# Tail of a fused two-layer graph network: bias on GpSimd, statistics and verdict ahead of the aggregation's copies, last evictions in another order

## Chip, cores and metric

The kernel runs on one core of a Trainium2 chip. The metric is the device time of one launch in microseconds, as the median of several runs. Engines are named as in the profile: PE is TensorE (PEld its weight loads), DVE is VectorE, ACT is ScalarE, POOL is GpSimd, SP is SyncE, which issues the DMAs here. A "q" behind an engine's name is its instruction queue.

## What is computed

The input is 32 graphs of 512 nodes with 512 features each. Layer 0 is masked attention with 8 heads of 64, layer 1 is a graph convolution with a dense 512 x 512 adjacency. Both add their input and normalise each node's features to mean 0 and variance 1.

```python
def _L0_gnn_ref(x, adj, Wq, bq, Wk, bk, Wv, bv):
    ...
    scores = jnp.einsum('bihd,bjhd->bhij', q, k) / jnp.sqrt(jnp.float32(HD))
    mask = jnp.where(adj == 0, jnp.float32(-1000000000.0), jnp.float32(0.0))
    scores = scores + mask[None, None, :, :]
    weights = jax.nn.softmax(scores, axis=-1)
    out = jnp.einsum('bhij,bjhd->bihd', weights, v)
    ...
def _L1_gnn_ref(x, adj, weight, bias):
    y = jnp.einsum('nm,bmd->bnd', adj, x)
    out = jnp.einsum('bnd,do->bno', y, weight) + bias
...
x = _layernorm(x + _L0_gnn_ref(x, adj, L0_gnn_Wq, L0_gnn_bq, L0_gnn_Wk, L0_gnn_bk, L0_gnn_Wv, L0_gnn_bv), axis=-1)
x = _layernorm(x + _L1_gnn_ref(x, adj, L1_gnn_weight, L1_gnn_bias), axis=-1)
```

## The kernel before

Batch b is one graph, held as `X[b]`: 128 partitions, four blocks of rows (c = 0 to 3), 512 features. While batch b is in its attention, the projections of b + 1 and the graph convolution of b - 1 and b - 2 are woven into it; the program's order is written out by hand, so each engine runs its instructions in the order in which the code issues them, and waits on semaphores for its inputs. Only the end is of interest here, where nothing is left to weave in. There t = 31 is the last batch, and batch 30 is the one before it.

The matrix product with the weight in layer 1 is done by Strassen's scheme in seven products (units 1, 2, 5, 6, 7, 3, 4 in this order, 8 matmuls each). The function `convolve(b, i)` runs unit i and adds its bank of PSUM into quarters of `X[b]`: x11, x12 (left and right half of blocks 0 and 1), x21, x22 (of blocks 2 and 3). Unit 1 is also copied to a tile `mix` by ScalarE (L535); units 6 and 7 add their bank to `mix` on VectorE (L537), and GpSimd then adds `mix` to x12, and to x21 and x22 (L539). All other additions are on VectorE from PSUM (L541).

The end of the program, from L803 on, runs as follows.

- The last units of batch 30 are mixed with the normalisation of layer 0 of batch 31. For each block, ScalarE normalises (L446) and copies the rounded high part (L502), and VectorE subtracts it from the row for the low part (L503). `split_rows` does the latter two.
- `add_bias` (L506) adds the bias of layer 1 to each of the four blocks, in place, on VectorE.
- `aggregate_rows` multiplies with the adjacency: 32 matmuls into four banks (L515), which ScalarE (L522, banks 0 and 2) and VectorE (L520, banks 1 and 3) copy to the tile `yT`. VectorE adds one more combination from banks 2 and 3 (L524), and GpSimd makes three further ones (`combine_rows`, L331 to L333).
- The list `last` then runs the seven units of batch 31. Beside them, by the table `beside`, run `seen` (the statistics of layer 1 of batch 30, L431 and L432, one pair for each block) and `old` (its normalisation: square root on ScalarE, L435; reciprocal and shift on VectorE, L440 and L441; four normalisations on ScalarE, L446). The finished batch 30 is stored by one DMA after unit 7 (L472).
- `judge` (L663 to L673) computes on VectorE whether all numbers stayed in range: three sums (L665 to L667), two comparisons (L669, L670) and two products (L671, L672). A matmul sums the outcome over the partitions at the very end (L859), and VectorE writes the verdict (L860).
- `half_statistics` (L832) computes the statistics of a half row of batch 31, and L849 merges two halves. Blocks 0 and 1 are finished after unit 3, blocks 2 and 3 after unit 4; each pair then gets its square root, reciprocal, shift, normalisation on ScalarE and a store for each block (L470).

After that each engine loads the verdict into a register (L201) and branches on it (L203). If it says so, a slower general kernel runs; otherwise the program closes with a barrier over all engines (shown at L881).

Of the kernel before, what the change touches and what calls it, by code (L numbers as in the profile page):

```python
# [37 lines left out]
FP = mybir.dt.float32  # L38
# [4 lines left out]
ALU = mybir.AluOpType  # L43
# [4 lines left out]
P = 128  # L48
# [16 lines left out]
def load_row(nc, pool, v, name):  # L65
    t = pool.tile([P, v.shape[0]], FP, name=name)
    nc.sync.dma_start(t, bass.AP(tensor=v.tensor, offset=v.offset, ap=[[0, P], [1, v.shape[0]]]))
    return t
# [139 lines left out]
def fast_kernel(ctx: ExitStack, tc, verdict, x, adj, Wq, bq, Wk, bk, Wv, bv, W1, b1, out):  # L208
    nc = tc.nc
    B, N, D = x.shape  # L210
    H = Wq.shape[1] // HD
    HP = H // 2
    NB = N // P
# [5 lines left out]
    work = ctx.enter_context(tc.tile_pool(name="work", bufs=2))  # L219
# [3 lines left out]
    def bank(*shape):  # L223

        return psum.tile([P, *shape], FP, name="bank", tag="bank", bufs=8)


    X, IN = {}, {}
    half = N // 2
# [40 lines left out]
    b1_r = load_row(nc, consts, b1, "b1_r")  # L270
# [57 lines left out]
    def combine_rows(t):  # L328

        a11, a12, a21, _, s1, s2, s4 = (t[:, i, :, :] for i in range(7))  # L330
        nc.gpsimd.tensor_sub(s2, s1, a11)  # L331
        nc.gpsimd.tensor_sub(a21, a11, a21)
        nc.gpsimd.tensor_sub(s4, a12, s2)  # L333
# [28 lines left out]
    def block_product(pm, t, w, i, turned=False):  # L362
        left, right = FACTORS[i]
        left, right = t[:, A_AT[left], :, :], w[:, B_AT[right], :, :]
        if turned:
            left, right = right, left
        for r in range(2):
            for d in range(2):
                nc.tensor.matmul(pm[:, r, :], left[:, d, r * P:(r + 1) * P], right[:, d, :],  # L369
                                 start=(d == 0), stop=(d == 1))  # L370
# [52 lines left out]
    STAT, RSTD, SHIFT, HIGH, LOW = {}, {}, {}, {}, {}  # L423
# [10 lines left out]
    def square_root(t, slots):  # L434
        nc.scalar.activation(RSTD[t][:, slots], STAT[t][:, slots, 1], AF.Sqrt, bias=eps)  # L435

    def invert_root(t, slots):

        rstd = RSTD[t][:, slots]
        nc.vector.reciprocal(rstd, rstd)  # L440
        nc.vector.scalar_tensor_tensor(SHIFT[t][:, slots], STAT[t][:, slots, 0], -1.0, rstd,  # L441
                                       op0=ALU.mult, op1=ALU.mult)

    def normalise(t, slot):
        row = X[t - slot // NB][:, slot % NB, :]
        nc.scalar.activation(row, row, AF.Identity, bias=SHIFT[t][:, slot:slot + 1],  # L446
                             scale=RSTD[t][:, slot:slot + 1])
# [20 lines left out]
    def store(b, blocks=None):  # L468
        for c in blocks or ():
            nc.sync.dma_start(out[b, c * P:(c + 1) * P, :], X[b][:, c, :])  # L470
        if blocks is None:
            nc.sync.dma_start(out[b].rearrange("(c p) d -> p c d", p=P), X[b])  # L472
# [6 lines left out]
    YT, MIX = {}, {}  # L479
# [23 lines left out]
        nc.vector.tensor_sub(low, row, high.bitcast(FP))  # L503

    def add_bias(b, c):
        nc.vector.tensor_add(X[b][:, c, :], X[b][:, c, :], b1_r)  # L506

    def aggregate_rows(b):

        yt = YT[b] = work.tile([P, 7, 2, half], FP, name="yT", bufs=1)  # L510
        banks = [bank(2, half) for _ in range(DB)]
        for c in range(NB):
            for d, pm in enumerate(banks):
                for part in (LOW[b, c], HIGH[b, c]):
                    nc.tensor.matmul(pm.rearrange("p a n -> p (a n)"), part[:, d * P:(d + 1) * P], adjT[:, c, :],  # L515
                                     start=(c == 0 and part is LOW[b, c]), stop=(c == NB - 1 and part is HIGH[b, c]))
        for d, pm in enumerate(banks):
            block = yt[:, d // 2:d // 2 + 3:2, d % 2, :]
            if d % 2:
                nc.vector.tensor_copy(block, pm)  # L520
            else:
                nc.scalar.activation(block, pm, AF.Copy)  # L522
            if d >= 2:
                nc.vector.tensor_add(yt[:, A_AT["S1"], d % 2, :], pm[:, 1, :], yt[:, A_AT["A21"], d % 2, :])  # L524
        combine_rows(yt)

    def convolve(b, i):

        pm = bank(2, half)
        block_product(pm, YT[b], w1, i)  # L530
        x11, x12, x21, x22 = (X[b][:, 2 * r:2 * r + 2, s * half:(s + 1) * half] for r in range(2) for s in range(2))
        if i == 1:

            MIX[b] = work.tile([P, 2, half], FP, name="mix", tag="q" if b >= B - 3 else "low", bufs=2)
            nc.scalar.activation(MIX[b], pm, AF.Copy)  # L535
        if i in (6, 7):
            nc.vector.tensor_add(MIX[b], pm, MIX[b])  # L537
            for block in (x12,) if i == 6 else (x21, x22) if b == B - 1 else (x22,):
                nc.gpsimd.tensor_add(block, block, MIX[b])  # L539
        for block in {1: (x11,), 5: (x12, x22), 2: (x11,), 3: (x12,), 4: (x21,)}.get(i, ()):  # L540
            nc.vector.tensor_add(block, pm, block)  # L541
        if i == 4 and b < B - 1:

            nc.gpsimd.tensor_add(x21, x21, MIX[b])
# [6 lines left out]
    def convolution(b):  # L551
        return [(convolve, b, i) for i in (1, 2, 5, 6, 7, 3, 4)] if b >= 0 else []
# [110 lines left out]
    def judge():  # L663
        seen = consts.tile([P, 3], FP, name="seen")
        nc.vector.tensor_reduce(seen[:, 0:1], sums, axis=AX.XY, op=ALU.add)  # L665
        nc.vector.tensor_reduce(seen[:, 1:2], inverses, axis=AX.XY, op=ALU.add)
        nc.vector.tensor_reduce(seen[:, 2:3], inexact, axis=AX.X, op=ALU.add)  # L667
        well = consts.tile([P, 3], FP, name="well")
        nc.vector.tensor_scalar(well[:, 0:2], seen[:, 0:2], BOUND, None, op0=ALU.is_le)  # L669
        nc.vector.tensor_scalar(well[:, 2:3], seen[:, 2:3], 0.0, None, op0=ALU.is_equal)  # L670
        nc.vector.tensor_mul(well[:, 0:1], well[:, 0:1], well[:, 1:2])  # L671
        nc.vector.tensor_mul(well[:, 0:1], well[:, 0:1], well[:, 2:3])  # L672
        return well[:, 0:1]  # L673


    def run(units):
        for unit in units:
            unit[0](*unit[1:])
# [15 lines left out]
    def norm(t, which):  # L694

        if t - which < 0:
            return []
        lo, hi = which * NB, (which + 1) * NB
        return [(square_root, t, slice(lo, hi)), (invert_root, t, slice(lo, hi))] + [
            (normalise, t, slot) for slot in range(lo, hi)]  # L700
# [4 lines left out]
    def survey(b):  # L705

        return [(statistics, b, 1, c) for c in range(NB)] if b >= 0 else []
# [95 lines left out]
    t = B - 1  # L803
# [4 lines left out]
    old, seen = norm(t - 1, 1), survey(t - 1)  # L808
# [11 lines left out]
    run(rest[3 + NB:])  # L820
    for c in range(NB):
        add_bias(t, c)
    aggregate_rows(t)


    halves = {}
    spare = work.tile([P, NB, 2, nc.vector.BN_STATS_DIM], FP, name="part", bufs=1)

    def half_statistics(c, s):
        if c not in halves:  # L830
            halves[c] = spare[:, c, :, :]
        nc.vector.bn_stats(halves[c][:, s, :], X[t][:, c, s * half:(s + 1) * half])  # L832

    old = norm(t, 1)
    beside = {1: seen, 2: old[:2], 5: old[2:3], 6: old[3:5], 7: old[5:]}
    for unit in last:
        run([unit] + beside.get(unit[2], []))
        if unit[2] == 2:
            well = judge()
        if unit[2] == 7 and t > 0:  # L840
            store(t - 1)
        for c, s in {2: ((0, 0), (1, 0)), 3: ((0, 1), (1, 1)), 4: ((2, 1), (3, 1), (2, 0), (3, 0))}.get(unit[2], ()):
            half_statistics(c, s)
            if (c < 2) == (s == 1):
                if t + 1 not in STAT:
                    for table, name, shape in ((STAT, "stat", (2 * NB, 2)), (RSTD, "rstd", (2 * NB,)),
                                               (SHIFT, "shift", (2 * NB,))):
                        table[t + 1] = work.tile([P, *shape], FP, name=name, bufs=3)
                nc.vector.bn_aggr(STAT[t + 1][:, NB + c, :], halves[c])  # L849
        ready = {3: (0, 1), 4: (2, 3)}.get(unit[2], ())  # L850
        if ready:
            slots = slice(NB + ready[0], NB + ready[1] + 1)
            square_root(t + 1, slots)
            invert_root(t + 1, slots)
            for c in ready:
                normalise(t + 1, NB + c)
                store(t, [c])
    pm = bank(N)
    nc.tensor.matmul(pm[0:1, 0:1], well, ones[:, 0:1], start=True, stop=True)  # L859
    nc.vector.tensor_scalar(verdict, pm[0:1, 0:1], P - 0.5, None, op0=ALU.is_lt)  # L860
# [24 lines left out]
```

## Time and profile before

| what | value |
|---|---|
| median of 4 runs | 2788.06 us (2787.47 to 2788.84) |
| the profiled execution's own time | 2788.24 us |
| its span, first to last instruction | 2786.4 us |
| granted TensorE clock | 0.996 |
| aggregation of batch 31 on TensorE (L515) begins | 2750.78 us |
| its seven units on TensorE (L369) | 2758.87 to 2771.83 us |
| last normalisation on ScalarE (L446) | 2778.63 + 0.80 us |
| last store issued | 2779.5 us |

Times in the profile count from the start of the span. A line of the timeline gives start, duration, engine, source line and operation, the tile written and those read, their shapes, and how many instructions were merged into the line; in brackets stands how long the engine had been idle before and what it waited for. Lines of a single source line give the count, the shortest, median and longest duration in ns, and the first and last start. Instructions of one engine overlap a little in these records[...].

### The profile page before, as it was taken

The page shows a single profiled execution, that of the slowest core. Times are in us where ns is not written, and L with a number is a line of the kernel's source. Part 1 is how long each engine was busy: PE and PEld are TensorE (multiplying, and loading weights), DVE is VectorE, ACT ScalarE, POOL GpSimd, SP SyncE. Part 2 cuts the span into 40 slices and gives each one's busy share as a digit, 9 for nine tenths or more (in the row PEclk, how much of TensorE's full clock was granted, in tenths as well). Part 3 has the DMA queues.
Part 4 walks back from the last instruction along what each step waited for, and adds up shares of the span by engine and source line. Part 5 has one row for each costly group of instructions (what it writes and reads, how often), then busy time and mean ns, then how long its engine had stood idle before and what let it go on. Part 6 is the DMA issues. An engine that isn't in the chain of part 4 may idle for free. (4 is left out here: it accounts for less than half of the span.)

```text
span 2786.4 us, 39215 instructions
## 1 busy us (share of the span) xinstructions
PE 2755.0 (99%) x12850; PEld 1920.6 (69%) x12850; DVE 2032.9 (73%) x3349; ACT 1406.0 (50%) x2447; POOL 1898.2 (68%) x1221
## 2 busy tenths in 40 slices
PE   9999999999999999999999999999999999999997
PEld 6666766767767667667676676676766766767755
DVE  6777676687776777767867667777677676687776
ACT  2455544654545555445545455464455544654554
POOL 4666776767766667676677676676666777767764
PEclk9999999999999999999999999999999999999999
DMA  5112212222122222122221222211222212222111
GB/s 146 29 31 57 44 29 56 60 60 55 23 50 57 61 56 42 31 56 60 58 57 19 53 59 60 56 28 45 56 61 57 43 30 56 60 59 56 32 36 48
DMA packets 588305, 141.66 MB, mean 51 GB/s; under 512 B 549952, under 2 KB 554048, under 8 KB 588096
## 3 DMA queue, kind: packets, MB, share of 16 engines
q1 hardware_dynamic: 588096, 139.10, 22.6%
q8 instruction: 103, 1.69, 0.3%
q14 instruction: 106, 0.87, 0.1%
HBM read 72.88 MB, written 33.55 MB: 38 GB/s over the span
## 5 line engine op out<-in xcount | busy, mean ns | idle before, releaser
L572 ACT ACTIVATE e<-e 128x1024 f32<-128x1024 f32 x512 | 524.1, 1052 | 541.8 <-DVE e L570 516.3
L583 POOL TENSOR_TENSOR es<-es,e 128x1024 f32<-128x1024 f32 x256 | 617.7, 2413 | 20.1
L570 DVE SCALAR_TENSOR_TENSOR e<-gap,bank 128x512 f32<-128x512 uint8 x1024 | 616.6, 675 | 12.2 <-PE bank L568 12.2
L583 POOL TENSOR_TENSOR es<-e 128x1024 f32<-128x1024 f32 x128 | 316.1, 2469 | 309.8 <-ACT e L572 309.8
L568 PE MATMUL bank<-q,k 64*128 64x512 f32 x2048 | 476.2, 600 | 0.3 <-DVE attT L606 0.3
L592 PE MATMUL bank<-e,v 128*64 128x512 f32 x2048 | 457.3, 599 | 4.7 <-DVE v L404 4.7
L369 PE MATMUL bank<-wv,xT 128*128 128x256 f32 x1792 | 405.4, 381 | 0.0
L369 PE MATMUL bank<-xT,wk 128*128 128x256 f32 x1792 | 403.0, 379 | 0.7 <-DVE wk L319 0.7
L369 PE MATMUL bank<-xT,wq 128*128 128x256 f32 x1792 | 403.0, 383 | 0.5 <-DMA wq<-in_L_gnn_Wq_dram 0.5
L568 PEld LDWEIGHTS bank<-q,k 64*128 64x128 f32 x2048 | 212.3, 186 | 262.7 <-issue 136.5
L369 PE MATMUL bank<-w,yT 128*128 128x256 f32 x1792 | 392.3, 379 | 0.5 <-DVE yT L520 0.5
L369 PEld LDWEIGHTS bank<-w,yT 128*128 128x128 f32 x1792 | 340.4, 190 | 47.8 <-DVE yT L520 0.9
L369 PEld LDWEIGHTS bank<-xT,wk 128*128 128x128 f32 x1792 | 340.5, 190 | 46.8 <-PE bank L369 1.1
L369 PEld LDWEIGHTS bank<-xT,wq 128*128 128x128 f32 x1792 | 339.9, 191 | 47.0 <-issue 0.9
L369 PEld LDWEIGHTS bank<-wv,xT 128*128 128x128 f32 x1792 | 337.8, 190 | 47.0 <-DVE e L570 0.8
L592 PEld LDWEIGHTS bank<-e,v 128*64 128x64 f32 x2048 | 142.5, 138 | 284.7 <-issue 278.3
L650 ACT ACTIVATE rows<-rows,zero,inverse 128x64 f32<-128x64 f32 x992 | 335.0, 427 | 3.5 <-DMA rows<-attT 3.4
L651 POOL TENSOR_TENSOR xs<-xs,rows 128x512 f32<-128x512 f32 x122 | 154.6, 1289 | 187.5 <-DMA xs<-in_x_dram 187.5
L572 ACT ACT_TABLE_LOAD x31 | 39.8, 1283 | 419.5 <-DVE e L570 419.5
L541 DVE TENSOR_TENSOR xs<-bank,xs 128x512 f32<-128x512 f32 x186 | 120.0, 672 | 157.1 <-ACT mix L535 156.9
L491 ACT ACTIVATE yT<-bank 128x512 f32<-128x512 f32 x124 | 74.0, 598 | 291.2 <-PE bank L488 291.2
L446 ACT ACTIVATE xs<-xs,shift,rstd 128x512 f32<-128x512 f32 x248 | 181.9, 803 | 27.2 <-DVE shift L441 25.7
(123 smaller groups left out, 3025.9 us busy)
## 6 DMA issues: line engine op xcount, KB each, us to landing
xin<-in_x_dram SPq DMA_DIRECT2D x496, 64.0 KB, 2.4
xs<-in_x_dram SPq DMA_DIRECT2D x31, 1024.0 KB, 5.1
rows<-attT SPq DMA_DIRECT2D x1984, 16.0 KB, 1.8
out_dram<-xs SPq DMA_DIRECT2D x31, 1024.0 KB, 4.4
xin<-in_x_dram SPq DMA_DIRECT2D x4, 256.0 KB, 3.6
wq<-in_L_gnn_Wq_dram SPq DMA_DIRECT2D x2, 512.0 KB, 6.9
wk<-in_L_gnn_Wk_dram SPq DMA_DIRECT2D x2, 512.0 KB, 8.4
yT<-in_adj_dram SPq DMA_DIRECT2D x1, 1024.0 KB, 7.5
```

The costliest lines, as they stand in the source:

```text
L369: nc.tensor.matmul(pm[:, r, :], left[:, d, r * P:(r + 1) * P], right[:, d, :], start=(d == 0), stop=(d == 1))
L446: nc.scalar.activation(row, row, AF.Identity, bias=SHIFT[t][:, slot:slot + 1], scale=RSTD[t][:, slot:slot + 1])
L491: nc.scalar.activation(yt[:, d // 2:d // 2 + 3:2, d % 2, :], pm, AF.Copy)
L541: nc.vector.tensor_add(block, pm, block)
L568: nc.tensor.matmul(ps[s], keys[:, j * P:(j + 1) * P], queries, start=True, stop=True)
L570: nc.vector.scalar_tensor_tensor(e[:, s, :], gap[:, j, :], NEG * root, ps[s], op0=ALU.mult, op1=ALU.add)
L572: nc.scalar.activation(e, e, AF.Exp, scale=1.0 / root)
L583: nc.gpsimd.tensor_add(ES[b, hp], ES[b, hp] if j > 1 else E[b, hp, 0], E[b, hp, j])
L592: nc.tensor.matmul(po[s * HD:(s + 1) * HD, :], values, e[:, s, :], start=(j == 0), stop=(j == NB - 1))
L650: nc.scalar.activation(part, part, AF.Identity, bias=zero, scale=inverse[:, c, s:s + 1])
L651: nc.gpsimd.tensor_add(cols, cols, rows)
```

## The change

Four edits, all in code that runs once, at the end.

1. `add_bias` runs on GpSimd.
2. The statistics of batch 30 (`seen`) and `judge` are issued in front of `aggregate_rows`, where they stand between `add_bias` and the copies on VectorE: two blocks' statistics, the verdict's seven operations, the other two blocks' statistics. The square root of batch 30 moves from unit 2 to unit 1.
3. In unit 7 of the last batch, the sum goes to a second `mix` tile.
4. The statistics, roots and normalisations of batch 31 are put in another order: unit 4's addition is issued ahead of the reciprocal of blocks 0 and 1, each of blocks 2 and 3 is closed on its own, and the last block is normalised by VectorE with one `tensor_scalar`. Blocks 2 and 3 are stored by two DMAs after that.

```diff
@@ -503,7 +503,7 @@
         nc.vector.tensor_sub(low, row, high.bitcast(FP))
 
     def add_bias(b, c):
-        nc.vector.tensor_add(X[b][:, c, :], X[b][:, c, :], b1_r)
+        nc.gpsimd.tensor_add(X[b][:, c, :], X[b][:, c, :], b1_r)
 
     def aggregate_rows(b):
 
@@ -534,7 +534,11 @@
             MIX[b] = work.tile([P, 2, half], FP, name="mix", tag="q" if b >= B - 3 else "low", bufs=2)
             nc.scalar.activation(MIX[b], pm, AF.Copy)
         if i in (6, 7):
-            nc.vector.tensor_add(MIX[b], pm, MIX[b])
+            mixed = MIX[b]
+            if i == 7 and b == B - 1:
+
+                MIX[b] = work.tile([P, 2, half], FP, name="mix", tag="q", bufs=2)
+            nc.vector.tensor_add(MIX[b], pm, mixed)
             for block in (x12,) if i == 6 else (x21, x22) if b == B - 1 else (x22,):
                 nc.gpsimd.tensor_add(block, block, MIX[b])
         for block in {1: (x11,), 5: (x12, x22), 2: (x11,), 3: (x12,), 4: (x21,)}.get(i, ()):
@@ -820,6 +824,9 @@
     run(rest[3 + NB:])
     for c in range(NB):
         add_bias(t, c)
+    run(seen[:2])
+    well = judge()
+    run(seen[2:])
     aggregate_rows(t)
 
 
@@ -831,30 +838,41 @@
             halves[c] = spare[:, c, :, :]
         nc.vector.bn_stats(halves[c][:, s, :], X[t][:, c, s * half:(s + 1) * half])
 
+    def close(c):
+        nc.vector.bn_aggr(STAT[t + 1][:, NB + c, :], halves[c])
+
+    for table, name, shape in ((STAT, "stat", (2 * NB, 2)), (RSTD, "rstd", (2 * NB,)), (SHIFT, "shift", (2 * NB,))):
+        table[t + 1] = work.tile([P, *shape], FP, name=name, bufs=3)
     old = norm(t, 1)
-    beside = {1: seen, 2: old[:2], 5: old[2:3], 6: old[3:5], 7: old[5:]}
+    beside = {1: old[:1], 2: old[1:2], 5: old[2:3], 6: old[3:5], 7: old[5:]}
+    upper, lower = slice(NB, NB + 2), slice(NB + 2, 2 * NB)
     for unit in last:
         run([unit] + beside.get(unit[2], []))
         if unit[2] == 2:
-            well = judge()
+            for c in range(2):
+                half_statistics(c, 0)
         if unit[2] == 7 and t > 0:
             store(t - 1)
-        for c, s in {2: ((0, 0), (1, 0)), 3: ((0, 1), (1, 1)), 4: ((2, 1), (3, 1), (2, 0), (3, 0))}.get(unit[2], ()):
-            half_statistics(c, s)
-            if (c < 2) == (s == 1):
-                if t + 1 not in STAT:
-                    for table, name, shape in ((STAT, "stat", (2 * NB, 2)), (RSTD, "rstd", (2 * NB,)),
-                                               (SHIFT, "shift", (2 * NB,))):
-                        table[t + 1] = work.tile([P, *shape], FP, name=name, bufs=3)
-                nc.vector.bn_aggr(STAT[t + 1][:, NB + c, :], halves[c])
-        ready = {3: (0, 1), 4: (2, 3)}.get(unit[2], ())
-        if ready:
-            slots = slice(NB + ready[0], NB + ready[1] + 1)
-            square_root(t + 1, slots)
-            invert_root(t + 1, slots)
-            for c in ready:
-                normalise(t + 1, NB + c)
-                store(t, [c])
+        if unit[2] == 3:
+            for c in range(2):
+                half_statistics(c, 1)
+                close(c)
+            square_root(t + 1, upper)
+    invert_root(t + 1, upper)
+    for c in range(2):
+        normalise(t + 1, NB + c)
+        store(t, [c])
+    for c in (2, 3):
+        half_statistics(c, 1)
+        half_statistics(c, 0)
+        close(c)
+    square_root(t + 1, lower)
+    invert_root(t + 1, lower)
+    normalise(t + 1, NB + 2)
+    row = X[t][:, 3, :]
+    nc.vector.tensor_scalar(row, row, STAT[t + 1][:, NB + 3, 0:1], RSTD[t + 1][:, NB + 3:NB + 4],
+                            op0=ALU.subtract, op1=ALU.mult)
+    store(t, [2, 3])
     pm = bank(N)
     nc.tensor.matmul(pm[0:1, 0:1], well, ones[:, 0:1], start=True, stop=True)
     nc.vector.tensor_scalar(verdict, pm[0:1, 0:1], P - 0.5, None, op0=ALU.is_lt)
```

## The prediction

> **What bounds the kernel now.** I read the page first, then the timeline of the last 40 us engine by engine, then the views of single lines for the end of the program.
>
> ```profile
> span 2786.4 us, 39215 instructions
> PE 2755.0 (99%) x12850; PEld 1920.6 (69%) x12850; DVE 2032.9 (73%) x3349; ACT 1406.0 (50%) x2447; POOL 1898.2 (68%) x1221
> ```
>
> TensorE is busy for 99% of the span, but no edit touches its work. Every edited line runs after the last block has been normalised and split, from 2756.8 us on, so only the last 30 us, 1% of the span, can change. VectorE there:
>
> ```profile
> 2755.48 1.37 DVE L503 TENSOR_TENSOR low<-xT,high 128x512 fp32r<-128x512 f32 x1 [0.56 <-ACT high L502]
> 2756.77 2.48 DVE L506 TENSOR_TENSOR xT<-xT,b_r 128x512 f32<-128x512 f32 x4
> 2759.18 0.68 DVE L520 COPY yT<-bank 128x512 f32<-128x512 f32 x1
> ...
> 2771.46 0.69 DVE L537 TENSOR_TENSOR mix<-bank,mix 128x512 f32<-128x512 f32 x1 [1.38 <-POOL xT L539]
> 2772.07 0.68 DVE L541 TENSOR_TENSOR xT<-bank,xT 128x512 f32<-128x512 f32 x1
> ...
> 2777.66 0.16 DVE L441 SCALAR_TENSOR_TENSOR shift<-stat,rstd 128x2 f32<-128x2 f32 x1
> 2777.74 0.14 DVE L860 TENSOR_SCALAR verdict<-bank 1x1 int32<-1x1 f32 x1
> ```
>
> The first copy of the aggregation (L520) stands behind the four bias adds, and TensorE waits for that copy:
>
> ```profile
> 2758.87 0.59 PE L369 MATMUL bank<-w,yT 128*128 128x256 f32 x2
> 2759.91 11.92 PE L369 MATMUL bank<-w,yT 128*128 128x256 f32 x54 [0.45 <-DVE yT L520]
> ```
>
> From R = 2759.91, 0.73 us after the copy's start, TensorE runs without a gap. The chain of waits follows VectorE on to the last two normalisations on ScalarE, ending at 2779.43. But 7 us follow that the chain doesn't explain. The views of the lines where the verdict is loaded (L201), branched on (L203) and the program closed (L881) do:
>
> ```profile
> L201 PEldq TENSOR_LOAD <-verdict x1: 485/485/485, 2777.9 to 2777.9; - x1
> L203 PEldq COMPARE_BRANCH  x1: 4278/4278/4278, 2778.5 to 2778.5; - x1
> L881 SPq DRAIN  x3: 7/7/7, 2784.2 to 2784.6; - x3
> L881 PEldq DRAIN  x2: 8/8/8, 2783.0 to 2786.2; - x2
> L470 SPq DMA_DIRECT2D out_dram<-xT x4: 332/341/351, 2775.6 to 2779.5; - x4
> ```
>
> TensorE loads the verdict as soon as VectorE has written it (2777.88), spends 4.28 us on the branch and drains a second time at 2786.2, 1.6 us after SyncE (2784.6), which waits for the output stores. The last event, 2786.4, comes from TensorE: it is **the verdict's end plus 8.5 us**. The stores have about 1.5 us of slack. So I count the time of the verdict first, the last store second.
>
> [...]
>
> ```profile
> 2694.39 1.27 POOL L332 TENSOR_TENSOR yT<-yT 128x512 f32<-128x512 f32 x1
> 2694.49 1.19 DVE L441 SCALAR_TENSOR_TENSOR shift<-stat,rstd 128x4 f32<-128x4 f32 x1
> ```
>
> L441 took 1.19 instead of 0.16 us, to the end of the GpSimd add. Statistics (L431: 0.66 to 0.68 beside GpSimd at 2762.75) and PSUM adds (L541: 0.68 at 2772.07) aren't slowed. L503 at 2755.48 was held by this too: GpSimd's add of 2755.00 ended at 2756.30, L503 0.55 later. [...]
>
> **The change part by part.** All from VectorE's list.
>
> *Bias to GpSimd.* VectorE loses four L506, 2759.18 - 2756.77 = 2.41 us before the copy. GpSimd gains four adds at 1.264 us (row L539 on xT, 128x512), free from 2756.30 until L331 at 2761.26. The first is stretched by 0.4[...] (an add of the same kind took 1.68 at 2751.32): 2756.3 to 2758.0, then 2759.2, 2760.5, 2761.7. Behind them in GpSimd's queue stand L331 to L333, which wait for L524 anyway; the first convolution's eviction needs the first two blocks, done by 2759.2. Cost there nothing; without that cover L331 would come up to 1 us late, and its reader, the fourth unit, has over 1 us to spare.
>
> *Statistics and verdict before the copies.* Four pairs of L431 and L432 at 0.795 (2762.75 to 2765.95 is 3.2 for four) = 3.18, and the seven operations of judge, 2766.81 to 2767.55 = 0.74. Sum 3.92, all on the path to the copy; their inputs are ready (last write to xs: L544, 2756.30). [...]
>
> [...] Two statistics end at 2758.36, so judge falls among the bias adds. Its last two, L671 and L672, have two SBUF inputs, and L672 reads L671. L671 would issue at 2758.83 and waits until 2759.25; L672 then finds the next add and waits until 2760.48. Two more pairs, 1.6: the copy starts at 2762.10, **2.92 us late**, R = 2762.83. The bounds are 1.51 (no block) and about 4.4: L669 and L670 are `tensor_scalar` on SBUF[...]; if both block too, they end at 2759.25 and 2760.48, L671 at 2761.72, L672 runs free, and the copy starts at 2763.6. I take 2.92[...].
>
> *Evictions.* VectorE gets rid of 3.9 us between the units. Units become ready every 11.92/54 x 8 = 1.766 us: the first at R + 1.60 (ScalarE's L535 at 2761.51), the sixth, unit 3, at R + 10.43, unit 4 at R + 12.2. Before, unit 3's add started at R + 12.16, after statistics, verdict and the wait of 1.38 for GpSimd to have read mix, which the second mix tile removes. Now VectorE meets it at R + 10.43. The old block's L441 then falls beside L333 and is blocked about 0.9, which units 5 to 7 absorb (VectorE is free by R + 7.8, unit 7 is ready at R + 8.67). From there: add and upper statistics to the square root 1.95 (2772.07 to 2774.02), R + 12.38; unit 4's add in its shadow, R + 12.25 to 12.87; reciprocal and shift 0.3 to R + 13.16; four half statistics and two aggregates 1.9 (1.87 before), R + 15.05; root 0.33, reciprocal 0.2, shift at R + 15.58. ScalarE normalises block 2 from R + 15.83 (0.25 after shift, as before) to R + 16.64; it has finished blocks 0 and 1 at R + 14.84. VectorE normalises block 3 beside it: [...]L524 took 0.41, so I take 0.43 as an estimate[...]. The verdict ends at R + 16.15, or 16.4.
>
> *Last stores.* Block 2's store is issued at R + 16.67, block 3's 0.71 later by SyncE's cadence (2778.75 to 2779.46), R + 17.38. So the normalisation on VectorE buys nothing there. The store of the whole block before (L472, 4.3 us to landing) moves with its normalisations from 2769.9 to about R + 8.3 and lands by R + 12.6, ahead of block 0's store at R + 14.1.
>
> *Sum.* The verdict was at R + 17.97 and comes at R + 16.15, 1.8 saved; R is 2.9 later: **+1.1 us**. The store was at R + 19.55, 2.17 saved, so +0.75, still under TensorE's end. The profiled execution took 2788.24 (span 2786.4 and 1.84 around it), 0.18 above the median; the same difference on the median gives 2788.06 + 1.1 = 2789.2.
>
> **The rivals.**
> - No block at judge: R +1.51, the verdict 0.3 earlier: 2787.8. [...] Against: L441 with four elements was blocked.
> - The `tensor_scalar` in judge block too: R +4.4, verdict +2.6: 2790.6.
> - Slower through starvation at one place, L503 of the last block: [...]it runs after three of them (2756.30 + 3 x 1.27 + 0.55 = 2760.65); then 3.92 follow, the copy starts at about 2764.5, 5.3 late, verdict +3.5: 2791.6. Each handover missed costs 1.27; the change is slower from a copy 1.8 us late. Against: at 2719.87 two L461 beside two long GpSimd adds each got in 0.55 us after one add's end. To pass 0.2% the copy would have to be 7.4 late, two more adds missed.
> - The close of the program changes: [...]the stores end it, about 1.45 us earlier: with +0.75 that is -0.7, 2787.4.
>
> **How the numbers follow.** Chances: forecast 0.45, no block 0.17, more blocks 0.23, starvation 0.06, other close 0.09. Forecast, no block and more blocks hold 0.85; with about 0.7 us of scatter of the runs (2787.47 to 2788.84) around their ends, the range is 2787.0 to 2791.2. 0.2%, 5.6 us, is about what a measurement of this kernel can tell from no change. No case reaches it alone: same 0.95; slower 0.04 for starvation that goes on through judge[...]; faster 0.01.
>
> **What would show it.** L506 gone from VectorE, four adds of about 1.27 on GpSimd from 2756.3, the first longer. L671 and L672 at about 0.4 and 1.2 instead of 0.16. L520 at 2762.1; TensorE's gap before it grown from 0.45 to about 3.4. No wait of L537 for L539. Unit 3's add 10.4 after R, the verdict's end 16.2 after R, and the last event 8.5 after the verdict. L520 at 2760.7 means no block; L503 longer than 1.4 means starvation; a last event elsewhere than 8.5 after the verdict breaks the step from verdict to end.

## The result and the profile after

The changed kernel is slower: 2791.96 us in the median of 40 runs (2789.77 to 2795.31) against 2788.09 us of the kernel before in 60 runs beside them. The ratio is 1.0014, with a 95% interval of 1.001 to 1.0019: 3.9 us where 1.1 were forecast, above the end of the range (2791.2).

The page of the changed kernel, in the same two lines as before:

```profile
span 2790.7 us, 39218 instructions
PE 2755.6 (99%) x12850; PEld 1921.2 (69%) x12850; DVE 2034.1 (73%) x3346; ACT 1405.2 (50%) x2446; POOL 1903.7 (68%) x1225
```

Shares of busy time say nothing here, since only the last 1% of the span differs. VectorE's timeline of the last 35 us does. In the changed kernel, lines behind L533 have moved: the verdict's operations L669 to L672 are now L673 to L676, L537 and L541 are L541 and L545, the verdict L860 is L878, the program's close L881 is L899.

```profile
2755.38 1.36 DVE L503 TENSOR_TENSOR low<-xT,high 128x512 fp32r<-128x512 f32 x1 [0.56 <-ACT high L502]
2756.66 0.68 DVE L431 BATCH_NORM_STATS2 bnst<-xs 128x6 f32<-128x512 f32 x1
...
2758.51 0.65 DVE L673 TENSOR_SCALAR well<-seen 128x2 f32<-128x2 f32 x1
2759.07 0.14 DVE L674 TENSOR_SCALAR well<-seen 128x1 f32<-128x1 f32 x1
2759.19 1.18 DVE L675 TENSOR_TENSOR well<-well 128x1 f32<-128x1 f32 x1
2760.40 1.18 DVE L676 TENSOR_TENSOR well<-well 128x1 f32<-128x1 f32 x1
...
2763.12 0.66 DVE L520 COPY yT<-bank 128x512 f32<-128x512 f32 x1
...
2776.73 0.69 DVE L545 TENSOR_TENSOR xT<-bank,xT 128x512 f32<-128x512 f32 x1 [1.10 <-PE bank L369]
...
2781.90 0.54 DVE L873 TENSOR_SCALAR xT<-xT,stat,rstd 128x512 f32<-128x512 f32 x1
2782.35 0.14 DVE L878 TENSOR_SCALAR verdict<-bank 1x1 int32<-1x1 f32 x1
```

Three operations on one or two elements, L673, L675 and L676, take 0.65, 1.18 and 1.18 us beside the bias adds on GpSimd. L673 ends at 2759.16, L675 at 2760.37 and L676 at 2761.58; the second, third and fourth add end at 2759.13, 2760.35 and 2761.57. Those adds, and the same three operations in the kernel before:

```profile
2756.14 5.43 POOL L506 TENSOR_TENSOR xT<-xT,b_r 128x512 f32<-128x512 f32 x4
```

```profile
2767.08 0.17 DVE L669 TENSOR_SCALAR well<-seen 128x2 f32<-128x2 f32 x1
...
2767.28 0.16 DVE L671 TENSOR_TENSOR well<-well 128x1 f32<-128x1 f32 x1
2767.48 0.16 DVE L672 TENSOR_TENSOR well<-well 128x1 f32<-128x1 f32 x1
```

The first copy starts 7.74 us after the last L503 does; before, it was 3.70. And unit 3's addition (2776.73) now waits 1.10 us for TensorE. TensorE's timeline shows what became of it:

```profile
2758.75 0.59 PE L369 MATMUL bank<-w,yT 128*128 128x256 f32 x2
2763.83 14.52 PE L369 MATMUL bank<-w,yT 128*128 128x256 f32 x54 [4.49 <-DVE yT L520]
```

The gap has grown from 0.45 to 4.49 us, as the copy's delay makes it. But the same 54 matmuls that took 11.92 us take 14.52. TensorE shows no second wait behind the gap; the table of stretches (busy time of each engine, then the granted share of TensorE's clock) has the cause in the column PEclk:

```profile
core 0: us, PE busy (x) PEld busy (x) DVE busy (x) ACT busy (x) POOL busy (x), PEclk, DMA share, GB/s
2760.00:2764.00 4.00, 0.17 (x1) 0.17 (x2) 3.90 (x8) 0.00 (x0) 1.57 (x2) 0.79 0.00 0
2764.00:2768.00 4.00, 4.00 (x10) 3.19 (x11) 1.54 (x4) 0.78 (x2) 2.82 (x3) 0.50 0.01 2
2768.00:2772.00 4.00, 4.00 (x18) 3.40 (x17) 2.30 (x7) 1.24 (x2) 0.89 (x1) 0.86 0.00 0
2772.00:2776.00 4.00, 4.00 (x20) 3.54 (x19) 2.15 (x4) 1.69 (x3) 1.56 (x2) 1.00 0.34 126
```

In stretches of 0.4 us the share is 1.00 up to 2762.0, 0.50 from 2762.4 to 2768.8 and 1.00 again from 2769.2; 0.87 and 0.59 in the two between put the fall at 2762.3, in the gap, 3.0 us after TensorE's last matmul (2758.75 + 0.59), and the return at 2769.1. The table above gives the same: 0.79 over 4 us is half clock for the last 1.7 of them (0.21 x 4 / 0.5). TensorE worked at half rate from 2763.83 to 2769.1, which loses half of 5.3 us, 2.6: the whole difference of 14.52 and 11.92.

The lines of the verdict's load, the branch and the close:

```profile
L201 PEldq TENSOR_LOAD <-verdict x1: 487/487/487, 2782.5 to 2782.5; - x1
L203 PEldq COMPARE_BRANCH  x1: 4453/4453/4453, 2783.1 to 2783.1; - x1
L899 SPq DRAIN  x3: 7/7/7, 2788.5 to 2788.8; - x3
L899 PEldq EVENT_SEMAPHORE  x2: 51/51/51, 2788.7 to 2790.6; - x2
```

The program again ends on TensorE, at 2790.7, 8.2 us after the verdict (2782.49).

The sum, each term counted from the start of the last L503, where the two traces are still alike (2755.48 and 2755.38), to the end of the span, 30.9 us before and 35.3 after: TensorE resumes 4.0 us later (8.45 instead of 4.43), its units take 2.6 longer, the verdict comes 16.06 instead of 17.97 after it resumes if those 2.6 are taken out (-1.9), and the close is 0.3 shorter. Together 4.4. This length, called **the tail** below, is used beside the medians, because L503's start itself differs by up to 3 us between profiled executions (2754.4 to 2757.3) for reasons that lie before the edited code.

**The price could have been read in the profile before.** 66 us ahead of that L503 stands a gap of the same kind, first in TensorE's timeline, then in the table of stretches of the kernel before:

```profile
2689.15 1.17 PE L488 MATMUL bank<-adjT,low 128*128 128x512 f32 x4 [2.88 <-DVE low L461]
```

```profile
2686.00:2690.00 4.00, 1.12 (x6) 0.75 (x5) 3.30 (x6) 0.60 (x1) 3.38 (x3) 1.00 0.68 242
2690.00:2694.00 4.00, 4.00 (x12) 1.72 (x12) 0.42 (x1) 1.93 (x3) 1.21 (x2) 0.57 0.02 4
```

After 2.88 us of waiting the clock was halved for 3.4 of the next 4 us (0.43 x 4 / 0.5). The row of clock tenths on the profile's page doesn't show it: a slice of it is 70 us long. It would have been a warning and no certainty: other profiles show the same gap without the price (see the gap filled by half, below).

### The profile page after: what moved, and what is told of

Read it like the earlier page. It is cut to its first block, busy times and chain, and to the rows that moved or that the text cites. A ratio compares the mean times of both kernels' runs of the same rounds, so it can differ in the third digit from the quotient of the medians.

```text
span 2790.7 us, 39218 instructions
## 1 busy us (share of the span) xinstructions
PE 2755.6 (99%) x12850; PEld 1921.2 (69%) x12850; DVE 2034.1 (73%) x3346; ACT 1405.2 (50%) x2446; POOL 1903.7 (68%) x1225
## 5 line engine op out<-in xcount | busy, mean ns | idle before, releaser
L545 DVE TENSOR_TENSOR xs<-bank,xs 128x512 f32<-128x512 f32 x186 | 120.1, 672 | 157.1 <-ACT mix L535 156.9
```

## The experiments

Theory: the copies are late by the moved statistics and by what the verdict's operations wait for GpSimd's adds (2.52 us in the profile above), less the bias adds, the gap of 4.49 us halves TensorE's clock, and the end follows the verdict through TensorE's branch (4.45 us) and the close behind it. Rivals stand in each expectation. Each run's median is given with that of the kernel before, run beside it on the same chip, and the ratio's 95% interval. Scatter of about 1 us in every kernel makes differences below that a matter of the profile alone.

**The gap filled.** In `aggregate_rows` of the changed kernel, behind the matmuls:

```diff
+        idle = bank(N)
+        for n in range(16):
+            nc.tensor.matmul(idle, HIGH[b, NB - 1][:, 0:P], adjT[:, NB - 1, :], start=True, stop=True)
         for d, pm in enumerate(banks):
```

> The changed kernel with 16 matmuls of 128x512 into an unread bank behind the aggregation, so that TensorE works through most of the 4.5 us gap; nothing is left out, work is added. Theory (TensorE's clock is halved after the gap): the 54 matmuls of the seven units take 11.9 us again instead of 14.5, no stretch at half clock, time 2.6 us under the changed kernel, about 2789.4 us. Rival (the units are slow because their operands from GpSimd and VectorE come late): the 54 matmuls still take about 14.5 us and the time stays at 2792 us.

Measured: 2788.54 us beside 2787.78 (ratio 1.0003, 0.9994 to 1.0011): 0.8 above the kernel before, where the changed kernel is 3.9 above it. TensorE's timeline of this run:

```profile
2757.99 3.89 PE L519 MATMUL bank<-adjT,high 128*128 128x512 f32 x16
2761.72 0.59 PE L369 MATMUL bank<-w,yT 128*128 128x256 f32 x2
2763.16 11.92 PE L369 MATMUL bank<-w,yT 128*128 128x256 f32 x54 [0.84 <-DVE yT L523]
```

The 54 matmuls are back at 11.92 us and PEclk is 1.00 in every stretch from 2760 to 2772, with the copy as late as in the changed kernel and the same operands from GpSimd and VectorE. The rival falls. The gain is larger than 2.6, though. In this profile TensorE's second drain (2785.6) also follows SyncE's (2785.5) at once, and the 16 added matmuls have moved the code behind them. Two later runs, with the code moved, part that off.

**The verdict back behind unit 2.** In the changed kernel:

```diff
-    run(seen[:2])
-    well = judge()
-    run(seen[2:])
+    run(seen)
     aggregate_rows(t)
...
         if unit[2] == 2:
+            well = judge()
             for c in range(2):
```

> The changed kernel with the verdict's seven operations back behind unit 2, the four statistics still ahead of the copies. Theory[...]: no operation with two SBUF inputs stands on VectorE beside the bias adds, the first copy starts near 2759.8, the gap of TensorE is about 1.2 us, its clock stays full, the verdict comes 16.1 after TensorE resumes at 2760.6; 1.2 to 1.5 us under the kernel before, about 2786.7 us. Rival (the statistics themselves are what costs[...]): the copy comes 0.8 us earlier than in the changed kernel, the time falls by no more than 1 us to 2791 us.

Measured: 2787.41 beside 2787.78 (0.9998, 0.999 to 1.0006), 0.4 us under the kernel before, where the changed kernel is 3.9 above it. VectorE's copy starts at 2759.90, 4.5 us after L503, and TensorE's gap is short:

```profile
2760.61 11.92 PE L369 MATMUL bank<-w,yT 128*128 128x256 f32 x54 [1.23 <-DVE yT L520]
```

The clock stays full and the verdict comes 16.07 us after TensorE resumes, as forecast. The rival, that the statistics themselves are what costs, falls. The gain on the kernel before is smaller than the 1.2 to 1.5 expected and not told apart from none; the tail is 30.3 against 30.9. Counted from L503, the verdict comes 1.1 us earlier than in the kernel before, but the close behind it takes 9.0 us instead of 8.5. The place of these seven short operations thus accounts for all that the change loses.

**The bias back on VectorE.** One word in `add_bias` of the changed kernel:

```diff
-        nc.gpsimd.tensor_add(X[b][:, c, :], X[b][:, c, :], b1_r)
+        nc.vector.tensor_add(X[b][:, c, :], X[b][:, c, :], b1_r)
```

> The changed kernel with the bias back on VectorE, all else as changed. Theory: [...] (0.5 in L673, 1.0 in each product) falls away, 2.4 us of bias adds come back, so the copy again starts at 2763.0, the gap of TensorE is 4.4 us and its clock is halved as before: within 0.5 us of the changed kernel, 2791.7 us. Rival (GpSimd's adds hold up the seven units as well): 2 us and more under the changed kernel, 2789.5 us.

Measured: 2791.94 beside 2787.78 (1.0016, 1.001 to 1.0023), the changed kernel's time. VectorE's timeline:

```profile
2756.81 2.48 DVE L506 TENSOR_TENSOR xT<-xT,b_r 128x512 f32<-128x512 f32 x4
...
2761.07 0.17 DVE L673 TENSOR_SCALAR well<-seen 128x2 f32<-128x2 f32 x1
...
2761.28 0.16 DVE L675 TENSOR_TENSOR well<-well 128x1 f32<-128x1 f32 x1
2761.47 0.16 DVE L676 TENSOR_TENSOR well<-well 128x1 f32<-128x1 f32 x1
...
2763.16 0.66 DVE L520 COPY yT<-bank 128x512 f32<-128x512 f32 x1
```

With no add on GpSimd beside them, the three operations are short again (0.17, 0.16 and 0.16 us), and the copy starts at the same time. The move of the bias takes 2.4 us off VectorE and gives 2.5 back in the three operations that wait for its adds on GpSimd (0.48 + 1.02 + 1.02). Here the clock was halved for less of the units (PEclk 0.57 from 2764 to 2768, 1.00 from there): the 54 matmuls took 13.61.

**The verdict early in the kernel before.** The matmul and the comparison move from the end into the loop:

```diff
-        if unit[2] == 7 and t > 0:
+        if unit[2] == 7:
             store(t - 1)
+            pm = bank(N)
+            nc.tensor.matmul(pm[0:1, 0:1], well, ones[:, 0:1], start=True, stop=True)
+            nc.vector.tensor_scalar(verdict, pm[0:1, 0:1], P - 0.5, None, op0=ALU.is_lt)
```

> The kernel before with the verdict's matmul and its comparison moved from the end to behind unit 7, nothing else changed. Theory[...]: TensorE branches after its last matmul at 2772.3 instead of 2778.5[...] and the program ends with the stores, about 1.5 us under the kernel before, 2786.6 us. Rival (the stores or the closing barrier set the end in any case): within 0.3 us of the kernel before.

Measured: 2785.78 beside 2787.78 (0.9993, 0.9987 to 1.0), 2.0 us less, with an interval that just reaches no change; the tail is 28.3, 2.6 less. The lines of the branch and the close:

```profile
L203 PEldq COMPARE_BRANCH  x1: 3335/3335/3335, 2773.2 to 2773.2; - x1
L881 SPq DRAIN  x3: 7/7/7, 2782.8 to 2783.1; - x3
L881 PEldq DRAIN  x2: 8/8/8, 2776.8 to 2783.4; - x2
```

TensorE branches 5 us earlier and its second drain stands 0.3 us behind SyncE's, no longer 1.6. The chain of waits of the kernel before had ended on ScalarE's last normalisation; what set the end was the verdict. The gain in the tail is larger than the 1.5 expected because the last store, issued 24.0 us after L503 in both kernels, landed 2.7 us after its issue and not 3.9; why wasn't tested.

**The bias alone.** The kernel before with `add_bias` on GpSimd, the first of the change's four edits and no other.

> The kernel before with the bias of the last batch on GpSimd and nothing else. Theory: VectorE waits for the bank instead of adding the bias, the first copy starts near 2758.1 instead of 2759.2, TensorE resumes near 2758.85, all that follows keeps its distance to it, the verdict comes 1.06 us earlier: about 2786.8 us. Rival (GpSimd's adds delay its three combinations, or its adds block the copies): the verdict no earlier than before, 2787.8 us.

Measured: 2788.37 beside 2789.00 (0.9999, 0.999 to 1.0007). The copy starts 2.64 us after L503 instead of 3.70, exactly the 1.06 forecast. TensorE then has no gap at all: its own matmuls of the aggregation now end last, so that unit 1 is ready only 0.7 us earlier, and the verdict, too, comes 0.7 earlier after L503 and not the 1.06 expected. The tail is 29.7, 1.2 less than before, but about half of that is a close of 7.9 us instead of 8.5, not the bias; the medians can't tell either.

**The order alone.** The changed kernel with the bias on VectorE, and in its table and loop:

```diff
-    run(seen[:2])
-    well = judge()
-    run(seen[2:])
     aggregate_rows(t)
...
-    beside = {1: old[:1], 2: old[1:2], 5: old[2:3], 6: old[3:5], 7: old[5:]}
+    beside = {1: seen, 2: old[:2], 5: old[2:3], 6: old[3:5], 7: old[5:]}
...
         if unit[2] == 2:
+            well = judge()
```

> The kernel before with the second mix tile, the new order of the evictions and the last block's normalisation on VectorE; bias on VectorE, statistics and the verdict's seven operations behind the copies as before. Theory: VectorE, still loaded with statistics and verdict between the units, reaches unit 3 1.2 us after it is ready, the verdict comes 17.3 after TensorE resumes instead of 18.0: 0.65 us under the kernel before, 2787.1 us. Rival (the gain of the order comes whole without moving statistics and verdict): 16.1 after, 1.9 us under, 2785.9 us.

Measured: 2788.01 beside 2789.00 (0.9997, 0.9989 to 1.0006), tail 30.4, 0.5 less, with the verdict 17.3 us after TensorE resumes. So the theory's size, not the rival's, but again below what the medians tell.

**The code moved, in the kernel before and in the changed one.** Behind the verdict's matmul, where TensorE has nothing to do:

```diff
     nc.tensor.matmul(pm[0:1, 0:1], well, ones[:, 0:1], start=True, stop=True)
+    spill = bank(N)
+    for n in range(16):
+        nc.tensor.matmul(spill[0:1, 0:1], well, ones[:, 0:1], start=True, stop=True)
```

> The kernel before with 16 more one-column matmuls on TensorE behind the verdict's matmul, while TensorE waits for the verdict; they only move the code behind them. Theory[...]: with the code moved the second drain follows the barrier at once, the program ends about 1.4 us earlier, 2786.4 us. Rival (the wait is part of the barrier): second drain still 1.6 us after the other engines, 2787.8 us.

> The changed kernel with 16 more one-column matmuls on TensorE behind the verdict's matmul, which fill no gap and only move the code behind them. It parts the gain of the filled gap (3.4 us under the changed kernel) into its two causes. Theory[...]: TensorE's gap and the halved clock stay[...], 1.4 us under the changed kernel, 2790.6 us, and the filled gap is worth the other 2 us. Rival (the whole gain of the filled gap was the moved code): 3.4 us under, 2788.6 us.

Measured in the kernel before: 2787.83 beside 2789.00 (0.9994, 0.9986 to 1.0003), tail 29.5, 1.4 less; the interval of the times includes no change. The close in that run:

```profile
L884 SPq DRAIN  x3: 7/7/7, 2783.1 to 2783.4; - x3
L884 PEldq DRAIN  x2: 8/8/8, 2781.8 to 2783.5; - x2
```

TensorE's wait of 1.6 us behind SyncE's last drain is gone, with nothing changed but the place of the code. What TensorE waited for was not shown. The trace of the kernel before lists two transfers of kind "instruction" of 16 KB on queue q8 there, one up to 2781.3, 1.5 us before TensorE's branch ends, and one from 2783.8 to 2784.7, 1.5 us ahead of its second drain.

Measured in the changed kernel: 2791.84 beside 2788.40 (1.0012, 1.0005 to 1.0018), tail 33.4 against 35.3, with the gap (4.50) as it was and the units still slow (14.13, 0.4 less than in the changed kernel's first profile). Its median is only 0.3 under that of the changed kernel run beside it (the third run below), so on the time the 1.4 is not confirmed; in the profiles it is, beside the 0.4 of the units. The rival, that moved code made the whole gain of the filled gap, falls. The filled gap's run has a tail 2.0 us shorter than this one (31.4), and this is the clock's part; by the medians, each against the kernel before beside it, it is 2.7 (0.8 against 3.4).

**The gap filled by half.** `range(8)` instead of `range(16)` in the first experiment's edit; and beside it **the changed kernel again**.

> The changed kernel with 8 instead of 16 matmuls of 128x512 in TensorE's gap, so that some 2.8 us of it stay empty. Theory[...]: the clock stays full, the 54 matmuls take 11.9 us, the time is that with 16 matmuls, 2788.5 us[...]. Rival[...]: 14 us for the 54 matmuls, 2791 us.

> The changed kernel itself, for a second profile and times from the same chip as the other two. Theory: the gap of about 4.5 us is there again and the clock is halved again, for 3.4 or 6.8 us, as the profiles of the changed kernel (6.8) and of the one with the bias on VectorE (3.4) showed, 2792 us. Rival (the halved clock was a chance of one execution): 54 matmuls in 11.9 us and 2789.4 us.

Measured with 8: 2789.65 beside 2788.40 (1.0005, 0.9996 to 1.0013), the 13 executions between 2787.58 and 2791.51. TensorE's timeline and the table of stretches:

```profile
2762.88 13.49 PE L369 MATMUL bank<-w,yT 128*128 128x256 f32 x54 [2.68 <-DVE yT L523]
```

```profile
2760.00:2764.00 4.00, 1.32 (x4) 0.94 (x4) 3.93 (x9) 0.00 (x0) 0.61 (x1) 0.83 0.00 0
2764.00:2768.00 4.00, 4.00 (x15) 3.33 (x14) 1.00 (x3) 0.78 (x2) 3.72 (x3) 0.74 0.01 2
```

My expectation failed: with a gap of 2.68 us the clock fell too. Reckoned as above (0.83 over 4 us is half clock for the last 1.4 of them) it fell at 2762.6, 2.4 us after TensorE's last matmul, where it was 3.0 in the changed kernel, and cost 1.6 us of the 54 matmuls. The changed kernel again: 2792.17 beside 2788.40 (1.0015, 1.0009 to 1.0022), with a gap of 4.50 and 14.36 us for the 54 matmuls. The halved clock wasn't a chance of one execution: with a gap of 4.4 to 4.5 us it came in all four profiles.

With a shorter gap it can be chance. The gap of 2.9 us some 66 us ahead of the last L503, before any edited code, stands in all 13 profiles of this case. In nine of them the clock was halved in it or within 1.2 us after it. In four (the gap filled, the gap filled by half, the code moved in the kernel before, the combined kernel) it stayed full; here in the run with 8 matmuls:

```profile
2688.75 1.17 PE L488 MATMUL bank<-adjT,low 128*128 128x512 f32 x4 [2.89 <-DVE low L461]
```

```profile
2684.00:2688.00 4.00, 1.86 (x8) 1.14 (x7) 3.90 (x9) 0.60 (x1) 3.92 (x3) 1.00 0.63 225
2688.00:2692.00 4.00, 3.25 (x14) 1.91 (x16) 1.36 (x3) 1.09 (x2) 1.36 (x2) 1.00 0.11 41
```

So one profile with a gap of 2.68 us shows that the clock can fall there, not that it always does.

**What the runs point to, combined.** The changed kernel with the verdict's operations and the statistics spread over VectorE's waits, and the verdict's matmul and comparison behind unit 7 as above:

```diff
         run(ahead[2 + c:3 + c] + rest[3 + c:4 + c])
+        if c == 2:
+            well = judge()
+        if c == 3:
+            run(seen[:1])
         split_rows(t, c)
...
-    run(seen[:2])
-    well = judge()
-    run(seen[2:])
+    run(seen[1:2])
     aggregate_rows(t)
...
+    beside = {1: seen[2:3], 2: seen[3:] + old[:1], 5: old[1:3], 6: old[3:5], 7: old[5:]}
...
-        if unit[2] == 2:
+        if unit[2] == 5:
             for c in range(2):
                 half_statistics(c, 0)
```

> Bias on GpSimd and the new evictions as changed; the verdict's operations and one block's statistics in the waits of VectorE ahead of the last two splits, one block's ahead of the copies, two behind units 1 and 2; the verdict's matmul and comparison behind unit 7. Theory: TensorE resumes near 2758.8 with full clock, the last store is issued 16.9 later near 2775.7, TensorE's branch is long done, and the program ends 4.4 after the last store: 6 us under the kernel before, about 2781.7 us. Rival (the parts get in each other's way: VectorE is late for unit 3[...]): no more than 3 us under, 2785 us.

Measured: 2783.75 beside 2789.00 (0.9983, 0.9976 to 0.999): faster than both kernels, by 5.2 us than the one before. The tail is 25.8, 5.1 less, though L503 starts some 0.2 later in it, counted from ScalarE's copy (L502) that it waits for. VectorE's timeline and TensorE's:

```profile
2752.74 0.40 DVE L673 TENSOR_SCALAR well<-seen 128x2 f32<-128x2 f32 x1
2753.05 0.14 DVE L674 TENSOR_SCALAR well<-seen 128x1 f32<-128x1 f32 x1
2753.17 0.16 DVE L675 TENSOR_TENSOR well<-well 128x1 f32<-128x1 f32 x1
...
2755.78 1.19 DVE L503 TENSOR_TENSOR low<-xT,high 128x512 fp32r<-128x512 f32 x1
...
2758.26 0.69 DVE L520 COPY yT<-bank 128x512 f32<-128x512 f32 x1 [0.48 <-PE bank L515]
```

```profile
2758.99 8.80 PE L369 MATMUL bank<-w,yT 128*128 128x256 f32 x40
```

The verdict's operations fit into a wait for ScalarE, one block's statistics into the time that L503 had spent beside GpSimd's add (1.37 us in the kernel before, 1.19 here, 0.69 for the block ahead of it), and TensorE has no gap. The 6 us expected were 5.2: TensorE went on as forecast, but the last store was issued at 2776.5, 17.5 us later and not 16.9, and the program ended 5.1 after it and not 4.4.

## Why the prediction was wrong

- **What bounds the tail:** right. Only the last 30 us changed, and the end follows the verdict, 8.2 us behind it. The early verdict and the moved code show both parts of it, the branch (3.34 us, from 2773.2) and TensorE's second drain (0.1 us behind SyncE's).
- **Bias to GpSimd:** right. Four adds in 5.43 us from 2756.14, the first stretched, and no cost for what stood behind them.
- **Statistics and verdict ahead of the copies, 3.92 us:** right. With the bias on VectorE the copy starts 6.35 us after the first bias add, 2.41 + 3.94.
- **The verdict's operations beside the bias adds:** that they are held was right, the size not. That `tensor_scalar` on one and two elements is not held was my estimate, which no row of the trace had shown. L673, on two, was held for 0.48; L674 came as one add gave way to the next, so its 0.14 shows nothing for one element; and both products then met a fresh bias add, 1.02 each. Sum 2.52 instead of 1.41: the copy came 4.0 late, not 2.92, inside the bounds (1.51 to 4.4) that the text had. The first rival, no block at judge, is refuted by the two products, on one element each.
- **Evictions:** the step that failed is "Units become ready every 11.92/54 x 8 = 1.766 us". It took TensorE's rate from the kernel before and set it behind a gap that the same text put at 3.4 us. Unit 3 was ready 12.9 us after TensorE resumed, not 10.43. With the clock full, the model holds: unit 3's add at 10.30 and the verdict at 16.06 after it in the run with the filled gap, against 10.43 and 16.15. No case of mine had the clock, which cost 1.6 to 2.6 us in four kernels; this put the time outside the range. Without it the terms of the sum above make 1.8 us (4.0 - 1.9 - 0.3), inside the range.
- **Normalisation on VectorE:** 0.54 us, between my estimate of 0.43, which no row of the trace had shown, and the 0.68 of a copy of 128x512 (L520), the other end. **Last stores:** the last came 0.43 after the one before it, not 0.71, to no effect on the end.
- **Rivals:** no starvation; L503 took 1.36 as before. More blocks at judge came true in part. The other close came true only in runs whose code was moved.

On the clock: it stood at half (PEclk 0.50) for 3.4 us in the kernel before (from 2690.2) and with the bias on VectorE (in the stretch from 2764), and for 6.8, twice that, in the changed kernel (from 2762.3). Behind the same gap of 2.9 us it was halved in nine profiles and not in four. No length of a single gap can be given as the limit: in the tail, gaps of 0.84 and 1.23 us left the clock alone, in one profile each, but in the run with the filled gap it was halved at 2703.9 (PEclk 0.58 from 2704 to 2708) behind a gap of 1.13 us at 2701, in a stretch where TensorE was busy for 2.87 of 4 us. What sets the limit stays open.

## What to carry to other kernels

A delay of the engine that feeds TensorE can have two prices: the delay, and the half-rate matmuls behind it, here 1.6 to 2.6 us. Small operations with two inputs in SBUF were not small here beside a busy GpSimd: each of the two products waited for the add that was running (1.18 us, 0.16 without it), and a `tensor_scalar` on two elements did so too (0.65 and 0.17). Put them where GpSimd rests. And look for what ends last past the end of the chain of waits: here a value that all engines branch on gained 2.6 us of tail by being written early, not last.

## What the runs showed of the hardware

- A gap of 2.68 us was enough to halve TensorE's clock in one profile, gaps of 4.37 to 4.50 did so in four of four, and one of 2.85 to 2.89 in nine of 13. It then cost half of the time worked until the clock was back, 1.6 us after the gap of 2.68 and 2.6 after one of 4.49.
- Beside GpSimd adds of 128x512 a VectorE `tensor_scalar` on 128x2 took 0.65 us (0.17 without them), and a product on 128x1 took 1.18 (0.16 without).
- With 16 matmuls more in front of it, TensorE's second wait at the close (1.6 us behind SyncE's last drain) was gone, and the tail was 29.5 us instead of 30.9 in the profiles.
- TensorE's branch at the end took 4.28 us in the kernel before, 4.45 in the changed one and 3.34 with the verdict early.
